# A state-space layer's inner loop on one Trainium2 core: the sums over states one scan later, softplus from one product, the skip term on VectorE, the gate multiplied by GpSimd

## The chip, the cores and the metric

One Trainium2 chip, one of its cores. The metric is the device time of the whole program in microseconds (us); here it is the median of three runs. A profile is one further execution taken by the hardware profiler. The engines are PE (TensorE, matmul), DVE (VectorE), ACT (ScalarE), POOL (GpSimd) and SP (SyncE, which here only issues DMAs). Each engine works through its own queue of instructions in order: an instruction that waits holds up all that stand behind it on that engine.

## What is computed

The program runs two transformer-like layers over 8 sequences of 1024 positions with 256 features, all in 32-bit floats. The first layer (mixture of experts, causal attention, mixture of experts) is not touched. The second is a channel mix, a selective state-space block and a second channel mix. The change is in the state-space block, cut here to what matters:

```
xz = in_proj_w @ h                       # h: normalised x; 2 x 512 channels
u, z = split(xz)
uc = silu(conv1d(u) + conv_b)            # causal, 4 taps, per channel
dt, Bm, Cm = split(x_proj_w @ uc)        # 64 + 16 + 16 rows
delta = softplus(dt_proj_w @ dt + dt_proj_b)
state[t] = exp(delta[t] * A) * state[t-1] + delta[t] * Bm[t] * uc[t]   # 512 channels x 16 states
y[t] = sum over the 16 states of state[t] * Cm[t]
y = (y + uc * D) * silu(z)
out = out_proj_w @ y + x
```

## The kernel before, in words

The second layer is `Layer1`. Its loop in `run` walks over `order`: 8 sequences b, of each 4 chunks c of 128 channels, of each chunk 16 steps k. One step holds 16 channels x 8 states on the 128 partitions and all 1024 positions along the free axis; two successive steps hold the two halves of the 16 states of the same channels. 8 x 4 x 16 makes 512 steps. Per step:

- SP fetches delta and delta*uc of 16 channels from DRAM, each row spread over 8 partitions (`fetch`, L1618; one fetch for two steps, four steps ahead; three buffers each).
- POOL multiplies by B (`feed`, L1641, two steps ahead).
- ACT computes exp(delta*A) into PSUM (`decay`, L1650, one step ahead; two buffers, so that a decay has to wait until the step two before it has been multiplied by C).
- DVE scans over the positions (L1744) and multiplies by C into `hc` (L1749; six buffers).
- Every fourth step PE adds the last four `hc` over their states into `py` (`add_up`, L1672), one PSUM tile `y` for the chunk. Before the first of these sums of a chunk a product with a diagonal matrix, `through` = D on the diagonal, made by ACT at L1757, puts uc*D into `py` (L1663).
- At step k = 1 of the next chunk, `close` multiplies `py` by silu(z), tile `zs`, into `uc` (L1683, DVE).

All other work of the layer is woven into this loop as side work. It consists of generators that yield before each small step with a rough cost (`need`): `steps_before` (mix, normalisation, projection and convolution of the next sequence), `steps_low` (B, C and the first delta of the next sequence), `steps_gate` (delta of the next chunk, then silu(z) of this one), and `steps_behind` (output projection and second mix of the sequence before). `Steps.turn` is called twice in each step of the loop and takes what is due by rates that are fixed when a list is added; `gap` is a least number of turns between two steps of a list. `drain` empties a list at once; the delta lists are drained at k = 12, where the fetches for the next chunk begin. PE products of side work use two PSUM banks (`bank`), which ACT or DVE empties one product later (`Pipe`).

Softplus is in `steps_delta`. It is computed as max(p, 0) + ln(1 + e) with e = exp(-|p|), and the rounding error of 1 + e is put back: with s = 1 + e rounded, ln s - ((s - 1) - e). The product p is made twice: first for Abs (L1466, ACT), and again at the end for the maximum (L1457 PE, L1480 DVE). In between, for each half of the 1024 positions, ACT makes s, ln s and s - 1 (L1473 to L1475) and POOL subtracts twice (L1477, L1478). One buffer of `sp1` holds s of a half. At last POOL makes du = delta*uc (L1486), and delta and du are sent to DRAM (`sent`, L1494).

The order in which add_up and the two turns stand in a step is this, before the change:

```python
            side.turn(0.5)
            if i % self.Q == 0 and i:
                add_up()
            nc.vector.tensor_tensor_scan(
                decays[i], decays[i], inputs.pop(i), 0.0, ALU.mult, ALU.add
            )
            side.turn(0.5)
            hc = pools["hc"].tile([P, T], F32, name="hc")
```

Of the kernel before, what the change touches and what calls it, by code (L numbers as in the profile page):

```python
# [8 lines left out]
F32 = mybir.dt.float32  # L9
BF16 = mybir.dt.bfloat16  # L10
I32 = mybir.dt.int32
AF = mybir.ActivationFunctionType
ALU = mybir.AluOpType
# [4 lines left out]
P = 128  # L18
# [27 lines left out]
class Net:  # L46


    def __init__(self, ctx, tc, B, T):
        self.tc, self.nc = tc, tc.nc  # L50
        self.B, self.T = B, T
        self.N = B * T
        self.NT = T // P
        self.C = self.N // P
        self.K = self.N // E
        self.KT = self.K // P
        nc = self.nc
        cp = ctx.enter_context(tc.tile_pool(name="consts", bufs=1))
        self.cp = cp
        self.ident = cp.tile([P, P], F32, name="ident")  # L60
        make_identity(nc, self.ident)
        self.ones = cp.tile([P, P], F32, name="ones")
        nc.gpsimd.memset(self.ones, 1.0)
        self.eps5 = cp.tile([P, 1], F32, name="eps5")
        nc.gpsimd.memset(self.eps5, 1e-5)
        self.eps6 = cp.tile([P, 1], F32, name="eps6")
        nc.gpsimd.memset(self.eps6, 1e-6)
# [439 lines left out]
class Attention:  # L507
# [5 lines left out]
    W = 512  # L513
# [418 lines left out]
    class Lists:  # L932
# [18 lines left out]
        def take(self, *kinds):  # L951

            for entry in self.lists:
                if entry[0] in kinds:
                    return self.step(entry)
# [106 lines left out]
class Layer1:  # L1062
# [9 lines left out]
    W = 512  # L1072
# [375 lines left out]
    def steps_delta(self, q, c, pools, pipe):  # L1448


        net, nc = self.net, self.net.nc
        T, W = net.T, self.W

        def offered(take):
            for t0 in range(0, T, W):
                pd = self.bank(pools, [P, W], "pd")
                nc.tensor.matmul(  # L1457
                    pd, self.w_dt[:, c * P : (c + 1) * P], q.xd[:, t0 : t0 + W],
                    start=True, stop=True,
                )  # L1460
                pipe.filled(lambda t0=t0, pd=pd: take(slice(t0, t0 + W), pd))

        yield need(pe=1.7, act=1.2)
        dl = pools["delta"].tile([P, T], F32, name="delta")
        e = du = pools["du"].tile([P, T], F32, name="du")
        offered(lambda t, pd: nc.scalar.activation(e[:, t], pd, AF.Abs))  # L1466
        yield need(act=1.1, banks=True)
        pipe.flush()
        nc.scalar.activation(e, e, AF.Exp, scale=-1.0)
        for t in (slice(0, W), slice(W, T)):  # L1470
            yield need(act=2.3, gap=2 if t.start else 0)
            e1 = pools["sp1"].tile([P, W], F32, name="sp_e1")
            nc.scalar.activation(e1, e[:, t], AF.Identity, bias=net.ones[:, 0:1])  # L1473
            nc.scalar.activation(dl[:, t], e1, AF.Ln)
            nc.scalar.activation(e1, e1, AF.Identity, bias=self.minus)  # L1475
            yield need(pool=2.5, gap=2)
            nc.gpsimd.tensor_tensor(e1, e1, e[:, t], ALU.subtract)  # L1477
            nc.gpsimd.tensor_tensor(dl[:, t], dl[:, t], e1, ALU.subtract)  # L1478
        yield need(pe=1.7, dve=1.4, gap=2)
        offered(lambda t, pd: nc.vector.scalar_tensor_tensor(  # L1480
            dl[:, t], pd, 0.0, dl[:, t], ALU.max, ALU.add
        ))
        yield need(banks=True, gap=1)
        pipe.flush()
        yield need(pool=2.3, gap=1)
        nc.gpsimd.tensor_tensor(du, dl, q.uc[c], ALU.mult)  # L1486
        q.steps[c] = self.sent(pools, "dl", c, dl)
        yield need(gap=1)
        q.du[c] = self.sent(pools, "du", c, du)
# [109 lines left out]
    def run(self, pools, load, load_x, keep_x, store):  # L1599
        net, nc = self.net, self.net.nc  # L1600
        T, W, B = net.T, self.W, net.B
        seqs = [self.Sequence(b) for b in range(B)]
# [51 lines left out]
        def add_up():  # L1654

            i0 = summed[0][0]
            b, c, _, _ = order[i0]
            first = i0 % NS == 0
            if first:
                self.py = pools["y"].tile([P, T], F32, name="y")  # L1660
            for t0 in range(0, T, W):
                if first:
                    nc.tensor.matmul(  # L1663
                        self.py[:, t0 : t0 + W], self.through,
                        seqs[b].uc[c][:, t0 : t0 + W], start=True, stop=False,
                    )
                for p in range(self.PARTS):
                    for i, hc in summed:
                        l, n = order[i][2:]
                        if n == p:  # L1670
                            g, j = divmod(l, self.RG // self.G)
                            nc.tensor.matmul(  # L1672
                                self.py[g * self.RG : (g + 1) * self.RG, t0 : t0 + W],
                                self.pick[:, j, :], hc[:, t0 : t0 + W], start=False,
                                stop=(j == self.RG // self.G - 1 and p == self.PARTS - 1),
                            )
            summed.clear()

        def close(i):

            b, c = order[i][:2]
            q = seqs[b]
            nc.vector.tensor_tensor(q.uc[c], self.py, q.zs, ALU.mult)  # L1683

        def before(b):

# [13 lines left out]
        side, pipe = self.Steps(), self.Pipe()  # L1700
# [12 lines left out]
        for i, (b, c, l, p) in enumerate(order):  # L1713
            k = i % NS
            if k == 2:
                if c == 0:
                    if b > 0:
                        side.drain("3behind")
                        side.add("3behind", behind(b - 1), 85, 56)
                    if b + 1 < B:  # L1720
                        side.add("2before", before(b + 1), 175, 48)
            if k == (0 if 0 < c < NDC - 1 else 2):
                side.add(
                    "1gate", self.steps_gate(seqs[b], c, pools, pipe),
                    *((30, 8) if c + 1 < NDC else (8, 2)),
                )
            if c == NDC - 1 and b + 1 < B and not seqs[b + 1].low:
                if k == 5:
                    side.drain("2before")
                if "2before" not in side.lists:  # L1730
                    seqs[b + 1].low = True
                    side.add("2low", self.steps_low(seqs[b + 1], pools, pipe), 33, 6)
            if k == NS - self.AHEAD:
                side.drain("1gate")
                if c == NDC - 1:
                    side.drain("2low")
            if p == 0:
                fetch(i + self.AHEAD)
            decay(i + 1)
            feed(i + 2)  # L1740
            side.turn(0.5)
            if i % self.Q == 0 and i:
                add_up()
            nc.vector.tensor_tensor_scan(  # L1744
                decays[i], decays[i], inputs.pop(i), 0.0, ALU.mult, ALU.add
            )
            side.turn(0.5)
            hc = pools["hc"].tile([P, T], F32, name="hc")
            nc.vector.tensor_tensor(hc, decays.pop(i), seqs[b].rep["c", p], ALU.mult)  # L1749
            summed.append((i, hc))  # L1750
            if (c, l) == (NDC - 1, lines[-1]) and b + 1 < B:
                rep(b + 1, "c", p)
            if k == 1:
                if i > 1:
                    close(i - 2)
                self.through = pools["through"].tile([P, P], F32, name="through")
                nc.scalar.mul(self.through, net.ident, self.skip[:, c : c + 1])  # L1757
        side.drain("3behind")
        add_up()
        close(len(order) - 1)  # L1760
# [5 lines left out]
def kernel(  # L1766
# [30 lines left out]
    nc = tc.nc  # L1797
    B, T, _ = x.shape
    net = Net(ctx, tc, B, T)
# [20 lines left out]
    with ExitStack() as st:  # L1820
        at = Attention(net, pool_in(st, "at_w", 1), w_qkv, w_out, b_out)
        with ExitStack() as ro:
            room = moe.room(ro)
            with ExitStack() as ph, tc.manual_schedule():
                pool, px = pool_in(ph, "f", 2), pool_in(ph, "f_x", B)
# [8 lines left out]
                while todo or works:  # L1834
                    if todo and len(works) < 2 and turn % 4 == 0:
                        b = todo.pop(0)
# [10 lines left out]
        with ExitStack() as ph:  # L1847
            at.places(pool_in(ph, "at_qk", 1), dram1)
            pools = {
                name: pool_in(ph, f"at_{name}", bufs) for name, bufs in (  # L1850
                    ("x", 3), ("xn", 2), ("xT", 1), ("side", 1), ("pT", 4), ("so", 2), ("oT", 2),
                    ("over", 2), ("sm", 2), ("junk", 1), ("r", 1), ("rT", 1),
                )
            }
# [14 lines left out]
    with ExitStack() as st:  # L1869
        w = pool_in(st, "l1_w", 1)  # L1870
# [4 lines left out]
        with tc.manual_schedule():  # L1875
            with ExitStack() as ro:
# [4 lines left out]
            name: pool_in(st, f"l1_{name}", bufs) for name, bufs in (  # L1881
                ("x", 2), ("mixT", 1), ("ka", 2), ("r", 2), ("hT", 2), ("u", 1), ("uc", 2 * NDC),
                ("xd", 1), ("delta", 1), ("du", 1), ("sp1", 1), ("zs", 1),
                ("rep", 1), ("sdl", 3), ("sdu", 3), ("dbu", 2), ("hc", 6), ("tap", 1), ("through", 1), ("xn", 2), ("small", 2),
            )
        }
        pools["dram"] = dram2
# [57 lines left out]
```

## Time and profile before

| what | value |
|---|---|
| median of 3 runs | 5593.31 us (5590.47 to 5599.83) |
| the profiled execution, its own time | 5598.68 us |
| its span in the profile | 5597.0 us |
| granted TensorE clock, mean over the span | 0.894 |
| first step's data of the second layer's loop | at about 2904 us |
| last chunk's gate | at 5524.84 us |
| one sequence of the loop, from 4237.28 to 4578.65 us | 341.37 us |

The span begins with the first instruction and ends with the last; 1.7 us of the execution's time lie outside it. A group in the profile is told by line, engine and operation, then output <- inputs by the program's names. Matmul records count more than the source: a product of 512 columns in 32-bit floats shows as two. The text speaks of steps as "c1 k4"; in the sequence of the table c0 k2 begins at 4237.28, c1 k0 at 4322.34, c2 k0 at 4405.17, c3 k0 at 4494.29, and c0 k2 of the next sequence at 4578.65 us.

### The profile page before, as it was taken

The page shows a single profiled execution, that of the slowest core. Times are in us where ns is not written, and L with a number is a line of the kernel's source. Part 1 is how long each engine was busy: PE and PEld are TensorE (multiplying, and loading weights), DVE is VectorE, ACT ScalarE, POOL GpSimd, SP SyncE. Part 2 cuts the span into 40 slices and gives each one's busy share as a digit, 9 for nine tenths or more (in the row PEclk, how much of TensorE's full clock was granted, in tenths as well). Part 3 has the DMA queues.
Part 4 walks back from the last instruction along what each step waited for, and adds up shares of the span by engine and source line. Part 5 has one row for each costly group of instructions (what it writes and reads, how often), then busy time and mean ns, then how long its engine had stood idle before and what let it go on. Part 6 is the DMA issues. An engine that isn't in the chain of part 4 may idle for free.

```text
span 5597.0 us, 60307 instructions
## 1 busy us (share of the span) xinstructions
PE 4612.8 (82%) x21302; PEld 2200.7 (39%) x21302; DVE 3432.3 (61%) x5654; ACT 2502.0 (45%) x4150; POOL 2202.1 (39%) x1801
## 2 busy tenths in 40 slices
PE   5699699999999997599767778787887878878767
PEld 5365434444444443356423233332433323333324
DVE  5532166666666773632117876777767677677884
ACT  2111145665566553011145556464564645545443
POOL 1244211111111111243226655666656555556662
PEclk7799889999999998699878889888898989989888
DMA  6123212212221222133134544536336364454642
GB/s 211 28 58 64 75 41 79 67 61 71 86 67 60 76 71 67 33 64 58 31 80 125 155 126 110 157 109 164 109 107 159 109 155 117 118 141 121 166 135 64
DMA packets 253568, 545.28 MB, mean 97 GB/s; under 512 B 30257, under 2 KB 144001, under 8 KB 253266
## 3 DMA queue, kind: packets, MB, share of 16 engines
q1 hardware_dynamic: 228690, 507.34, 32.2%
q0 software_dynamic: 24576, 34.10, 3.7%
q8 instruction: 168, 2.75, 0.2%
q14 instruction: 134, 1.10, 0.1%
HBM read 400.31 MB, written 141.03 MB: 97 GB/s over the span
## 4 chain that ended last, share of the span: by engine, by line
PE 26%; DVE 13%; ACT 6%; issue 5%; DMA 2%; POOL 1%; SPq 0%; DVEq 0%; POOLq 0%; ACTq 0%
DVE h L1744 8%; PE y L1672 5%; PE pc L1391 4%; PE pr L1286 4%; PE pk L1264 4%; PE pu L1442 2%; DVE hc L1749 2%; PE pp L1526 2%; ACT h L1650 2%; PE pd L1457 1%; ACT xn L1220 1%; PE pm L472 1%; PE px L1421 1%; DMA sdu<-du 1%; PE po L489 1%
## 5 line engine op out<-in xcount | busy, mean ns | idle before, releaser
L777 ACT ACTIVATE pT<-s 128x512 f32<-128x512 f32 (+3 forms) x1536 | 669.5, 489 | 520.2 <-PE s L734 510.8
L1650 ACT ACTIVATE h<-sdl,A 128x1024 f32<-128x1024 f32 x512 | 567.0, 1112 | 644.9 <-DVE hc L1749 623.2
L1672 PE MATMUL y<-hc,pick 128*32 128x512 f32 x2048 | 655.7, 723 | 226.9 <-DVE hc L1749 226.9
L734 PE MATMUL s<-kT,qT 32*128 32x512 f32 (+3 forms) x3072 | 828.6, 538 | 14.2 <-DVE mx L750 11.6
L1641 POOL TENSOR_TENSOR dbu<-sdu,b 128x1024 f32<-128x1024 f32 x256 | 602.0, 2352 | 409.2 <-DMA sdu<-du 215.1
L734 PE MATMUL s<-qT,kT 32*128 32x512 f32 (+3 forms) x3072 | 742.2, 538 | 7.7 <-ACT pT L777 7.7
L1744 DVE TENSOR_TENSOR_SCAN h<-h,dbu 128x1024 f32<-128x1024 f32 x256 | 586.0, 2289 | 184.7 <-ACT h L1650 158.8
L1744 DVE TENSOR_TENSOR_SCAN h<-h,sdu 128x1024 f32<-128x1024 f32 x256 | 586.1, 2289 | 159.6 <-ACT h L1650 146.4
L1749 DVE TENSOR_TENSOR hc<-h,c 128x1024 f32<-128x1024 f32 x512 | 625.5, 1222 | 31.5 <-PE y L1672 3.8
L783 POOL TENSOR_SCALAR_AFFINE_SELECT pT<-pT 128x512 f32<-128x512 f32 x256 | 162.4, 635 | 1137.0 <-ACT pT L777 1053.4
L1641 POOL TENSOR_TENSOR sdu<-sdu,b 128x1024 f32<-128x1024 f32 x256 | 602.4, 2353 | 15.8 <-DMA b<-bc 5.0
L734 PEld LDWEIGHTS s<-kT,qT 32*128 32x128 f32 x3072 | 318.9, 186 | 435.4 <-DVE mx L750 189.7
L476 ACT ACTIVATE mid<-pm,bu 128x512 f32<-128x512 f32 x192 | 131.6, 686 | 724.8 <-PE pm L472 714.7
L747 DVE TENSOR_REDUCE part<-s 128x1 f32<-128x512 f32 x512 | 329.1, 685 | 179.9 <-PE s L734 179.2
L1672 PEld LDWEIGHTS y<-hc,pick 128*32 128x32 f32 x2048 | 128.1, 126 | 718.8 <-issue 398.4
L497 POOL DMA_INDIRECT acc<-o,idx x128 | 207.1, 1618 | 496.0 <-DVE o L494 229.3
L750 DVE CUSTOM_DVE_ANT_0 junk<-s,mask,part 128x256 f32<-128x256 f32 (+3 forms) x512 | 281.5, 550 | 157.5 <-PE s L734 112.6
L472 PE MATMUL pm<-tT,wu 128*128 128x512 f32 x768 | 362.5, 609 | 0.0
L489 PE MATMUL po<-wd,mid 128*128 128x256 f32 x1536 | 350.1, 391 | 0.0
L750 DVE CUSTOM_DVE_ANT_0 junk<-s,mask 128x256 f32<-128x256 f32 (+3 forms) x512 | 250.5, 489 | 139.9 <-PE s L734 87.9
L797 PE MATMUL po<-pT,at_v 128*32 128x512 f32 (+3 forms) x3072 | 329.6, 501 | 0.7 <-POOL pT L783 0.4
L489 PEld LDWEIGHTS po<-wd,mid 128*128 128x128 f32 x1536 | 302.8, 198 | 44.5 <-issue 1.0
(262 smaller groups left out, 6703.8 us busy)
## 6 DMA issues: line engine op xcount, KB each, us to landing
sdl<-dl SPq DMA_DIRECT2D x256, 512.0 KB
sdu<-du SPq DMA_DIRECT2D x256, 512.0 KB
acc<-xt SPq DMA_DIRECT2D x24, 1024.0 KB
xt<-acc SPq DMA_DIRECT2D x24, 1024.0 KB
rows<-moe_r SPq DMA_DIRECT2D x16, 1056.0 KB
qT<-padded_q SPq DMA_DIRECT2D x32, 512.0 KB
kT<-padded_k SPq DMA_DIRECT2D x32, 512.0 KB
kept<-so SPq DMA_DIRECT2D x64, 256.0 KB
```

What stands on the lines that cost most here:

```text
L472: nc.tensor.matmul(pm, wu[:, k, n * P : (n + 1) * P], tT[:, k, t0 : t0 + HALF], start=(k == 0), stop=(k == KC - 1),)
L489: nc.tensor.matmul(po, mid[:, n, j * P : (j + 1) * P], wd[:, n, :], start=(n == 0), stop=(n == NF - 1),)
L734: self.net.nc.tensor.matmul(s[:, 0 : rhs.shape[-1]], lhsT, rhs, start=True, stop=True)
L747: nc.vector.tensor_reduce(part, sh, AX.X, ALU.max)
L750: nc.vector.tensor_tensor_reduce(junk[:, 0:w], sh[:, 0:w], self.mask[:, W - w : W], 1.0, part if a else -3e38, ALU.add, ALU.max, self.mx[n ...
L777: self.net.nc.scalar.activation(pT[:, h, 0:w], sh[:, 0:w], AF.Exp, scale=1.0 / HD**0.5)
L797: nc.tensor.matmul(q.po[h * HS : (h + 1) * HS, o:W], self.va[q.b % 2][:, j, g * HG + h, :], pT[:, h, 0 : W - o], start=(j == 0), stop=(j = ...
L1641: nc.gpsimd.tensor_tensor(inputs[i], t, seqs[b].rep["b", p], ALU.mult)
L1650: nc.scalar.activation(decays[i], spread["dl", i - p], AF.Exp, scale=self.A[:, p, n : n + 1])
L1672: nc.tensor.matmul(self.py[g * self.RG : (g + 1) * self.RG, t0 : t0 + W], self.pick[:, j, :], hc[:, t0 : t0 + W], start=False, stop=(j == ...
L1744: nc.vector.tensor_tensor_scan(decays[i], decays[i], inputs.pop(i), 0.0, ALU.mult, ALU.add)
L1749: nc.vector.tensor_tensor(hc, decays.pop(i), seqs[b].rep["c", p], ALU.mult)
```

## The change

Four edits, all in `Layer1`. The sums over states (`add_up`) are issued after the scan of their step and after the second turn. Softplus uses one product: ACT reads it for Abs and for Relu (into `dl`), the second product and the DVE operation go, and ACT and POOL work in four quarters in place of two halves, where one tile of `sp1` (of the same size, one buffer) now holds ln s and s - 1 of a quarter, and POOL adds ln s to the Relu as a third operation. The skip term leaves PE: DVE computes uc*D + py at the gate, and `through` goes. The multiplication by silu(z) follows on POOL. The `gap` values and costs of the softplus steps change with it.

```diff
-        self.ones = cp.tile([P, P], F32, name="ones")
+        self.ones = cp.tile([P, 1], F32, name="ones")
...
-        yield need(pe=1.7, act=1.2)
+        yield need(pe=1.7, act=2.4)
         dl = pools["delta"].tile([P, T], F32, name="delta")
         e = du = pools["du"].tile([P, T], F32, name="du")
-        offered(lambda t, pd: nc.scalar.activation(e[:, t], pd, AF.Abs))
-        yield need(act=1.1, banks=True)
+        for t0 in range(0, T, W):
+            pd = self.bank(pools, [P, W], "pd")
+            nc.tensor.matmul(
+                pd, self.w_dt[:, c * P : (c + 1) * P], q.xd[:, t0 : t0 + W], start=True, stop=True
+            )
+
+            def take(t=slice(t0, t0 + W), pd=pd):
+                nc.scalar.activation(e[:, t], pd, AF.Abs)
+                nc.scalar.activation(dl[:, t], pd, AF.Relu)
+
+            pipe.filled(take)
+        yield need(act=1.7, banks=True)
         pipe.flush()
         nc.scalar.activation(e, e, AF.Exp, scale=-1.0)
-        for t in (slice(0, W), slice(W, T)):
-            yield need(act=2.3, gap=2 if t.start else 0)
-            e1 = pools["sp1"].tile([P, W], F32, name="sp_e1")
-            nc.scalar.activation(e1, e[:, t], AF.Identity, bias=net.ones[:, 0:1])
-            nc.scalar.activation(dl[:, t], e1, AF.Ln)
-            nc.scalar.activation(e1, e1, AF.Identity, bias=self.minus)
-            yield need(pool=2.5, gap=2)
-            nc.gpsimd.tensor_tensor(e1, e1, e[:, t], ALU.subtract)
-            nc.gpsimd.tensor_tensor(dl[:, t], dl[:, t], e1, ALU.subtract)
-        yield need(pe=1.7, dve=1.4, gap=2)
-        offered(lambda t, pd: nc.vector.scalar_tensor_tensor(
-            dl[:, t], pd, 0.0, dl[:, t], ALU.max, ALU.add
-        ))
-        yield need(banks=True, gap=1)
-        pipe.flush()
+        w = W // 2
+        for t0 in range(0, T, w):
+            t = slice(t0, t0 + w)
+            yield need(act=1.2, gap=1 if t0 else 0)
+            e1 = pools["sp1"].tile([P, 2, w], F32, name="sp_e1")
+            nc.scalar.activation(e1[:, 0, :], e[:, t], AF.Identity, bias=net.ones[:, 0:1])
+            nc.scalar.activation(e1[:, 1, :], e1[:, 0, :], AF.Identity, bias=self.minus)
+            nc.scalar.activation(e1[:, 0, :], e1[:, 0, :], AF.Ln)
+            yield need(pool=2.2, gap=1)
+            nc.gpsimd.tensor_tensor(e1[:, 1, :], e1[:, 1, :], e[:, t], ALU.subtract)
+            nc.gpsimd.tensor_tensor(dl[:, t], dl[:, t], e1[:, 0, :], ALU.add)
+            nc.gpsimd.tensor_tensor(dl[:, t], dl[:, t], e1[:, 1, :], ALU.subtract)
         yield need(pool=2.3, gap=1)
         nc.gpsimd.tensor_tensor(du, dl, q.uc[c], ALU.mult)
...
             for t0 in range(0, T, W):
-                if first:
-                    nc.tensor.matmul(
-                        self.py[:, t0 : t0 + W], self.through,
-                        seqs[b].uc[c][:, t0 : t0 + W], start=True, stop=False,
-                    )
...
-                                self.pick[:, j, :], hc[:, t0 : t0 + W], start=False,
+                                self.pick[:, j, :], hc[:, t0 : t0 + W], start=(j == 0 and p == 0),
...
-            nc.vector.tensor_tensor(q.uc[c], self.py, q.zs, ALU.mult)
+            nc.vector.scalar_tensor_tensor(
+                q.uc[c], q.uc[c], self.skip[:, c : c + 1], self.py, ALU.mult, ALU.add
+            )
+            nc.gpsimd.tensor_tensor(q.uc[c], q.uc[c], q.zs, ALU.mult)
...
             side.turn(0.5)
-            if i % self.Q == 0 and i:
-                add_up()
             nc.vector.tensor_tensor_scan(
                 decays[i], decays[i], inputs.pop(i), 0.0, ALU.mult, ALU.add
             )
             side.turn(0.5)
+            if i % self.Q == 0 and i:
+                add_up()
...
-                self.through = pools["through"].tile([P, P], F32, name="through")
-                nc.scalar.mul(self.through, net.ident, self.skip[:, c : c + 1])
```

## The prediction

> **What bounds the kernel now.** I read the page first, then the waits and groups of one sequence in the middle of the second layer (4237.28 to 4578.65 us), then the chain of waits and the timelines inside it. The page's busy shares and the same shares for that sequence:
>
> ```profile
> PE 4612.8 (82%) x21302; PEld 2200.7 (39%) x21302; DVE 3432.3 (61%) x5654; ACT 2502.0 (45%) x4150; POOL 2202.1 (39%) x1801
> ```
> ```profile
> 4237.28:4578.65 341.37, 271.65 (x816) 118.38 (x816) 247.60 (x202) 182.17 (x243) 200.93 (x139) 0.89 0.49 130
> ```
>
> Of 341.4 us PE is busy 271.7, DVE 247.6, POOL 200.9, ACT 182.2 (then granted clock, DMA share, GB/s). Nobody is full: the loop is bound by engines that wait for each other in order. Scan and hc alone need 64 x (2.29 + 1.22) = 224.6 us of DVE, so a sequence cannot come much under 250. Who waits for whom (total us, times, longest):
>
> ```profile
> ACT h L1650 <- DVE hc L1749: 75.1, 30, 7.3
> DVE h L1744 <- ACT h L1650: 46.1, 14, 5.9
> POOL sp_e L1477 <- ACT sp_e L1475: 40.6, 6, 13.2
> PE y L1672 <- DVE hc L1749: 26.5, 9, 5.8
> ...
> POOL du L1486 <- DVE delta L1480: 17.1, 2, 9.4
> ...
> DVE uc L1683 <- PE y L1672: 11.6, 3, 7.2
> ...
> DVE delta L1480 <- PE pd L1457: 7.8, 3, 6.3
> ```
>
> DVE's dearest wait is for the next decay on ACT: 46.1 us. The first line is only a decay's two PSUM buffers, and costs nothing by itself. A decay is late when ACT stands before it with something else in hand: evicting a PE product, or softplus. So what counts is where the change puts work in ACT's queue, and when PE hands ACT its products.
>
> **What goes.** The groups of the sequence (count | busy us, mean ns of one):
>
> ```profile
> L1457 PE MATMUL pd<-xd,w_dt 97*128 97x512 f32 x32 | 17.4, 652 | 6.1 <-ACT ka L1272 4.6 <-DVE cm_r L1310 1.1 <-DVE xt L1530 0.3
> ...
> L1477 POOL TENSOR_TENSOR sp_e<-sp_e,du 128x512 f32<-128x512 f32 x8 | 10.2, 1270 | 40.6 <-ACT sp_e L1475 40.6
> ...
> L1663 PE MATMUL y<-uc,through 128*128 128x512 f32 x16 | 9.6, 685 | 1.2 <-ACT h L1650 1.2
> ...
> L1480 DVE SCALAR_TENSOR_TENSOR delta<-pd,delta 128x512 f32<-128x512 f32 x8 | 5.5, 686 | 8.3 <-PE pd L1457 7.8 <-POOL delta L1478 0.5
> ```
>
> PE loses half of pd (8.7 us) and all of through (9.6): 18.3 of 271.7. DVE loses 8 x 0.686 = 5.5. ACT loses four through of 0.393 (1.6) and the halves, 8 x (0.712 + 0.630 + 0.722) = 16.5. POOL loses 16 x 1.27 = 20.3. Most of PE's 18.3 lies beside other work; the chain of waits has these pieces of what goes: pd 1.98 and 0.88, through 1.05, 0.86 and 1.05, delta with its issue gaps 3.33, ACT's through 0.40. That is 9.55 us a sequence. One such place, c2 k4 to k6 (start, us, what):
>
> ```profile
> 4435.34 1.05 PE y L1672 x2
> 4436.38 1.05 PE y L1663 x2
> 4437.44 1.84 PE y L1672 x8
> 4439.28 7.07 PE pc L1391 x16
> 4446.35 0.88 PE pd L1457 x2
> 4447.25 0.69 DVE delta L1480
> ```
>
> **What comes.** ACT: 8 Relu from PSUM at 0.59 like Abs (4.7), and 16 quarters of Identity, Identity, Ln on 256 columns. No row has that size. Below, half of the 512 column times (1.03 a quarter); above, xn 128x256 at 0.594 each (1.78). From 512 to 1024 columns one ACT operation grows by about 0.43, so 256 is about 0.21 less than 512: 0.50 + 0.50 + 0.42 = 1.42. Sum 22.7; ACT nets +9.3 (bounds +3 to +15). POOL: 48 operations on 256 columns. Below, 0.55, which the one-input xt<-xt,n_up,n_off on 256 columns takes; above, 0.73 by the growth from 1.27 at 512 to 2.35 at 1024 columns; I take 0.73, as these have two inputs: 35.0. The gate multiply is as du, 1024 columns, 2.35: 9.4. POOL nets +24.1 (+16 below), to 225 of 341. DVE's gate changes from a two-input to a scalar-and-two-input operation: on 512 columns xt<-xt,pp takes 0.685 and cm_r<-pv,cm_r 0.678, so nothing, within 0.1. The DMAs stay: delta and du go out about as early in POOL's queue (du one feed earlier in c0 and c1), and SP's list is as long.
>
> **What is moved and who waits.** The orders in which the built programs hold their instructions give the rest; I laid the durations along them by hand.
>
> c1 (k0 to k8), a loss. In POOL's queue the gate multiply now stands ahead of the feed of k4, and the first quarter of softplus behind that feed. The multiply waits for DVE's close, and this for the sums; these now stand behind one more mix product (pk, 3.65 us) and end at about 4335.5 where they ended at 4332.0. So: close 4336.7, multiply 4339.0, feed 4341.3, first quarter 4343.4. ACT's second quarter needs the one `sp1` buffer, so it waits until then and ends at 4345. Behind it on ACT stand both sigmoid evictions, which PE has ready before that, and the decay of k4:
>
> ```profile
> 4342.62 0.60 ACT L1296 ACTIVATE cm_r<-pr 128x512 f32<-128x512 f32 x1 [1.58 <-PE pr L1286]
> 4343.24 1.28 ACT L1156 ACT_TABLE_LOAD   x1
> 4344.53 1.12 ACT L1650 ACTIVATE h<-sdl,A 128x1024 f32<-128x1024 f32 x1
> ```
>
> That decay ends at about 4350.0 in place of 4345.65: +4.4. Less the deltas and their wait there (1.8): **+2.6**. What was hidden here, POOL's 9.5 us of idle before its second half, is the cover that now decides.
>
> c2, about even. The gate multiply pushes POOL by 2.35, hidden behind ACT's table load and sigmoids (ACT wants the second quarter at 4431.3, POOL frees the buffer at 4429.2). But ACT's third quarter waits for POOL's second to about 4435, and tap, behind it, is ready at 4440 in place of 4438. PE has nothing then for 8.6 us, and the sums, issued later, cut into pc. The decay of k7 ends at about 4454 with a fast PE, against 4450.2 before; the delta waits gone (6.3 + 0.7) and PE's 3 us less pay most back by k9: -1.7. Here a rule speaks against the change. A pause of PE shows in the granted clock (third number from the end) of these windows:
>
> ```profile
> 4319.50:4324.10 4.60, 0.01 (x1) 0.00 (x0) 4.57 (x3) 2.24 (x3) 4.52 (x3) 0.97 0.33 91
> 4324.10:4326.20 2.10, 2.06 (x4) 0.56 (x6) 2.06 (x3) 1.11 (x2) 0.74 (x2) 0.50 0.85 207
> 4326.20:4332.00 5.80, 5.80 (x18) 1.25 (x17) 3.11 (x2) 5.66 (x8) 3.00 (x2) 0.62 0.49 127
> ```
>
> After 4.6 us without work PE ran at half speed for 2.1 + 0.76 x 5.8 = 6.5 us, which cost about 3.2. The Trainium skill (TensorE: Matmul & The Clock Gate, part 1, the HAM clock gate) says that PE drops to half rate after an idle window of about 3.4 us and needs about 3.4 us of work to come back: a cost of about 1.7. By the rule c2 gives -1.7 + 1.7 = 0, by the row +1.5; the row is this kernel's, I take **+1.2** as part hides. So less work on PE is partly paid in clock.
>
> c3, the gain. Before the sigmoids PE does pd 1.80, through 1.91 and the sums 3.7, then pr. Now through is gone and three quarters of pr stand ahead of the sums: pr ends 2.0 earlier, and ACT has its second softplus step (2.06) behind it in no case. The decay of k7 comes 4.1 earlier, deltas save 1.3, and POOL, with 4.4 us a step against DVE's 3.5, gives back 0.8: **-4.6**.
>
> c0, even. The quarters stand between the four xn of the mix: pp starts at about 4267.7, not 4264.15. The second pd (1.98) and the deltas after it (2.9) go, and the sums leave the front of pr; pr starts at 4296.9 against 4296.27: **+0.5**. The multiply hides under the 11 us in which POOL waits for a DMA.
>
> Sum: 2.6 + 1.2 - 4.6 + 0.5 = -0.3 a sequence, times 7: -2. The last sequence loses delta waits of 7.9 and 1.7 us and gains POOL locks of about 4 us in two chunks: about 0. At the very end the multiply stands alone before the output projection: +2.4. PE idles 18 us more a sequence; one further cold start, half of it on the path, is 1.6 x 8 = +13. Together +14: 5598.7 + 14 = 5612.7 against the profiled execution. The median of the runs is 5.4 below that execution, so 5593.3 + 14 = **5607**. About 0.2% (11 us) is what a measurement of this kernel can tell from no change.
>
> **The rivals.** *PE's relief decides.* All 9.55 us leave the chain and neither POOL nor the clock takes anything back, for which speaks that PE holds most of the chain: 8 x 9.55 = 76, 5517 (5500 to 5575). Against it: ACT's wait in c1 must not happen. *The one buffer decides, slower.* ACT's quarters wait for POOL, which waits for the gate. It decides where POOL ends its first quarter in c1 after the last sigmoid eviction could be done, 4343.2; from there each us of POOL is a us of the loop. With c1 +4.4, c2 +4.6, c0 +3.5 and less than half of c3's gain, +10 a sequence: 5673. *The later sums do nothing.* In c2 (pc, pd, sums, pr) they keep their neighbours, so the 7.2 us in which DVE waits for them at the gate stay. This is contained in the first sum, and moves it by no more than 2 us a sequence (16).
>
> **How the numbers follow.** The balance has 0.45 (own range 5580 to 5635), PE's relief 0.30, the buffer 0.25. In the balance's range about a third lies within 0.2%, a tenth below. Faster 0.34, same 0.16, slower 0.50. The range 5510 to 5680 leaves out some 0.1 on each side.
>
> **What would show it.** Right: a wait of ACT sp_e for POOL in every sequence (8.4 us in all of 3750 to 5500 before), longest in c1; POOL du no longer waiting for DVE; PE less busy by about 18 us a sequence at a lower mean clock; c3 shorter and c1 longer. Wrong: c1 not longer, or DVE's 46 us for decays fallen by a third; or PE's clock unchanged.

## The result, and the profile after

The kernel after takes 5615.59 us (median of 11 runs, 5602.99 to 5622.30) beside 5594.11 us before (11 runs, 5586.20 to 5605.51): a ratio of 1.0033, 95% interval 1.0023 to 1.0042. The medians lie 21.5 us apart; the ratio, taken over all runs, stands for about 18 us. The profiled execution after has a span of 5613.9 us, 16.9 more than the one before.

First the page's busy shares of the kernel after (us, share of the span, instructions), to be held against the first lines shown of before.

```profile
PE 4486.9 (80%) x21046; PEld 2169.7 (39%) x21046; DVE 3399.0 (61%) x5590; ACT 2562.8 (46%) x4374; POOL 2390.5 (43%) x2089
```

PE does 126 us less, DVE 33 less; ACT does 61 more and POOL 188 more. By busy shares the bound engine was relieved, and the time grew. The same sequence of the second layer, from k2 of its c0 to k2 of the next, in the row by windows with PE, PEld, DVE, ACT and POOL, then granted clock, DMA share and GB/s:

```profile
4256.60:4600.30 343.70, 259.16 (x784) 115.72 (x784) 243.41 (x194) 189.64 (x271) 223.93 (x175) 0.85 0.49 129
```

PE fell from 271.7 to 259.2 us, at a clock of 0.85 for 0.89. POOL rose from 200.9 to 223.9, ACT from 182.2 to 189.6. The length didn't fall: 343.7 for 341.4. Its waits (total us, times, longest):

```profile
DVE h L1738 <- ACT h L1648: 47.9, 16, 6.5
...
POOL uc L1679 <- DVE uc L1676: 39.2, 4, 16.6
...
ACT sp_e L1476 <- POOL delta L1482: 20.2, 6, 9.0
...
DVE uc L1676 <- PE y L1665: 15.0, 3, 7.2
```

DVE's waits for pd and POOL's for delta are gone, as the edit of softplus implies. DVE's wait for decays stayed (46.1, now 47.9, and the longest grew from 5.9 to 6.5). Two waits are new: POOL stands 39.2 us before the multiply of the gate, and ACT stands 20.2 us before a quarter of softplus until POOL gives the one buffer back. The second can hold up a decay, since decays are in ACT's queue; the first holds up what stands behind the multiply on POOL, a feed and the next quarter. The groups give the new operations' prices (count | busy us, mean ns of one | idle before them):

```profile
L1480 POOL TENSOR_TENSOR sp_e<-sp_e,du 128x256 f32<-128x256 f32 x16 | 11.6, 728 | 10.6 <-ACT sp_e L1477 10.6
...
L1476 ACT ACTIVATE sp_e<-du,ones 128x256 f32<-128x256 f32 x16 | 8.1, 504 | 20.3 <-POOL delta L1482 20.2
...
L1676 DVE SCALAR_TENSOR_TENSOR uc<-uc,skip,y 128x1024 f32<-128x1024 f32 x5 | 6.4, 1277 | 15.0 <-PE y L1665 15.0
```

The table below divides the second layer by the starts of its 512 scans. A sequence is counted from k2 of its c0 to k2 of the next c0; inside it, c0 is k2 to k15, c1 and c2 have 16 steps each, c3 has 16 and the next two. Chunk times are means of the six middle sequences.

| part, us | before | after | difference |
|---|---|---|---|
| until the first scan | 2919.0 | 2926.2 | +7.2 |
| first sequence | 290.8 | 301.9 | +11.1 |
| c0 | 85.0 | 84.1 | -0.9 |
| c1 | 82.9 | 86.9 | +4.1 |
| c2 | 89.1 | 87.7 | -1.4 |
| c3 | 84.4 | 82.7 | -1.8 |
| a middle sequence (six of them) | 341.4 | 341.5 | +0.1 |
| last sequence, k2 to its last scan | 250.9 | 247.1 | -3.8 |
| last scan to the end | 81.2 | 82.8 | +1.6 |

So six sequences break even, as a sum of a loss in c1 and gains elsewhere, and what is lost in all stands ahead of them. Of the +7.2 at the start, 3.5 is there before the first product of softplus: the first layer is the same in both programs, and in the profiles of the experiments below, which don't touch it either, the first scan came anywhere from 2914.4 to 2935.7 us. Single executions therefore can't settle the start.

### The profile page after: what moved, and what is told of

Read it like the earlier page. It is cut to its first block, busy times and chain, and to the rows that moved or that the text cites. A ratio compares the mean times of both kernels' runs of the same rounds, so it can differ in the third digit from the quotient of the medians.

```text
span 5613.9 us, 60312 instructions
## 1 busy us (share of the span) xinstructions
PE 4486.9 (80%) x21046; PEld 2169.7 (39%) x21046; DVE 3399.0 (61%) x5590; ACT 2562.8 (46%) x4374; POOL 2390.5 (43%) x2089
## 4 chain that ended last, share of the span: by engine, by line
PE 24%; DVE 9%; ACT 7%; POOL 5%; issue 5%; DMA 3%; SPq 0%; DVEq 0%; POOLq 0%; ACTq 0%
DVE h L1738 6%; PE y L1665 4%; PE pc L1391 4%; PE pk L1264 4%; PE pr L1286 3%; PE pu L1442 2%; ACT h L1648 2%; DMA sdu<-du 2%; PE pp L1524 1%; POOL dbu L1639 1%; DVE hc L1745 1%; PE pm L472 1%; PE px L1421 1%; ACT xn L1220 1%; ACT L1156 1%
## 5 line engine op out<-in xcount | busy, mean ns | idle before, releaser
L1665 PE MATMUL y<-hc,pick 128*32 128x512 f32 x2048 | 626.5, 706 | 237.8 <-DVE hc L1745 226.9
L1228 PE MATMUL tr<-ident,xn 128*128 128x128 f32 x384 | 96.9, 374 | 300.3 <-ACT xn L1220 276.1
```

The lines of the kernel that those rows point to most:

```text
L1665: nc.tensor.matmul(self.py[g * self.RG : (g + 1) * self.RG, t0 : t0 + W], self.pick[:, j, :], hc[:, t0 : t0 + W], start=(j == 0 and p == 0 ...
```

## The experiments

My theory after the result was that of the prediction: gains and a POOL lock that cancel. It had two claims that could fail: that the later sums were harmless or good, and that the lock in c1 was the multiply's. The rivals were that the later sums themselves lose, and that softplus or the gate loses by itself. So I made each of the three edits alone first. Each ran 4 to 21 times, beside before on the same chip (before's median 5600.65 for e1 to e4, and 5602.34 on another chip for e8 to e11); the profile, and so the chunk times, are of one execution each. Chunks are counted as in the table.

| kernel | median us | ratio to before (95%) | c0 | c1 | c2 | c3 | middle sequence | first sequence |
|---|---|---|---|---|---|---|---|---|
| before | 5594.11 | 1 | 85.0 | 82.9 | 89.1 | 84.4 | 341.4 | 290.8 |
| after | 5615.59 | 1.0033 (1.0023-1.0042) | 84.1 | 86.9 | 87.7 | 82.7 | 341.5 | 301.9 |
| e1 sums later, alone | 5649.45 | 1.0087 (1.0073-1.0101) | 83.7 | 84.0 | 95.8 | 84.4 | 347.8 | 295.9 |
| e2 softplus, alone | 5563.94 | 0.9933 (0.9919-0.9947) | 85.2 | 82.4 | 82.7 | 83.5 | 333.8 | 288.3 |
| e3 gate, alone | 5590.98 | 0.9981 (0.9974-0.9987) | 84.1 | 82.0 | 88.7 | 82.8 | 337.6 | 293.8 |
| e4 as e3, multiply on DVE | 5588.40 | 0.9976 (0.9967-0.9986) | 82.8 | 82.3 | 88.9 | 83.6 | 337.6 | 294.7 |
| e8 after, sums early | 5556.88 | 0.9916 (0.9902-0.9929) | 84.1 | 82.3 | 82.4 | 82.3 | 331.1 | 295.4 |
| e9 as e8, multiply on DVE | 5539.26 | 0.9887 (0.9872-0.9902) | 82.5 | 82.3 | 82.1 | 83.4 | 330.4 | 292.8 |
| e10 after, one sum early | 5581.96 | 0.9961 (0.9948-0.9975) | 83.7 | 86.8 | 81.8 | 82.5 | 334.8 | 301.1 |
| e11 after, multiply at k5 | 5591.12 | 0.9977 (0.9969-0.9986) | 84.3 | 83.3 | 87.7 | 82.6 | 338.0 | 295.3 |

**The later sums alone (e1).** Before, with one move:

```diff
-            if i % self.Q == 0 and i:
-                add_up()
             nc.vector.tensor_tensor_scan(
                 decays[i], decays[i], inputs.pop(i), 0.0, ALU.mult, ALU.add
             )
             side.turn(0.5)
+            if i % self.Q == 0 and i:
+                add_up()
```

> Before, with the sums alone issued one scan later (through and the second product stay). My theory (gains of PE in c3 are given back by waits of ACT for POOL and by what is exposed at the start): in c3 three quarters of pr now stand ahead of the sums and of through, so its evictions and the decay of k7 come about 4 us earlier in each of 7 sequences: about -25 us, 5569. Rival 'the later sums do nothing': within 8 us of 5594. Rival 'the later sums lengthen the wait at the gate': DVE uc <- PE y grows from 84 us by 3 us for most chunks and the time rises by 20 us or more.

Measured: 5649.45 us, slower by 0.87%. My expectation had the wrong sign. The rival of a longer wait at the gate had the sign, but not the place: that wait grew from 84.5 to 101.0 us in the whole program, while c2 alone grew by 6.7 us in each middle sequence; c1 grew by 1.1 and c3 not at all. PE's timeline of e1 in c2 (start, us, what, idle before):

```profile
4459.39 8.22 PE L1391 MATMUL pc<-u,tap 128*128 128x512 f32 x12 [5.68 <-ACT tap L1383]
4467.44 1.02 PE L1663 MATMUL y<-uc,through 128*128 128x512 f32 x2
...
4473.13 1.99 PE L1391 MATMUL pc<-u,tap 128*128 128x512 f32 x4
4474.95 2.06 PE L1457 MATMUL pd<-xd,w_dt 97*128 97x512 f32 x4
```

PE first waits 5.68 us for tap with nothing in its queue. Then through and the sums of k4, 5.7 us together, stand between the 12th and the 13th pass of pc, and pd behind that. DVE's timeline of e1 shows who pays:

```profile
4476.01 0.69 DVE L1480 SCALAR_TENSOR_TENSOR delta<-pd,delta 128x512 f32<-128x512 f32 x1 [13.07 <-PE pd L1457]
```

DVE stands 13.07 us for pd. Before, the sums lay ahead of pc (4437.44 and 4439.28 in the lines of the prediction), in a time in which PE had nothing else.

**Softplus from one product, alone (e2).** Before, with this part of the change (shortened here):

```diff
-            nc.gpsimd.tensor_tensor(dl[:, t], dl[:, t], e1, ALU.subtract)
-        yield need(pe=1.7, dve=1.4, gap=2)
-        offered(lambda t, pd: nc.vector.scalar_tensor_tensor(
-            dl[:, t], pd, 0.0, dl[:, t], ALU.max, ALU.add
-        ))
...
+                nc.scalar.activation(dl[:, t], pd, AF.Relu)
...
+            nc.gpsimd.tensor_tensor(dl[:, t], dl[:, t], e1[:, 0, :], ALU.add)
+            nc.gpsimd.tensor_tensor(dl[:, t], dl[:, t], e1[:, 1, :], ALU.subtract)
```

> Before, with softplus alone from one product, in quarters. My theory: PE loses 8.7 us and DVE 5.5 us a sequence, but the chain of quarters between ACT and POOL through one buffer is longer: +3.6 us at the start of the loop where nothing hides it, some +8 in sequence 0, which has little side work, and no gain in c1 or c2 of the others: together +5 to +20 us, about 5607. Rival 'PE's relief decides': -5 us a sequence, about 5555. Rival 'only the gate multiply ahead of the quarters makes them late': without it no loss, 5594 or less.

Measured: 5563.94 us, 0.67% faster. My own theory, a loss of 5 to 20 us, failed; 'PE's relief' with 5555 is near. A middle sequence gains 7.6 us, 6.4 of them in c2, where DVE no longer waits for a second pd. Of the waits of e2 in the same sequence, the one for the buffer of softplus:

```profile
ACT sp_e L1476 <- POOL delta L1482: 13.0, 6, 8.8
```

The quarters on one buffer make ACT wait 13.0 us already without any multiply on POOL, and it costs the loop nothing there: c1 is at 82.4 for 82.9.

**The gate, alone (e3, e4).** Before, with through gone, skip in DVE's operation at the gate, and the multiply on POOL in e3 (shortened):

```diff
-                if first:
-                    nc.tensor.matmul(
-                        self.py[:, t0 : t0 + W], self.through,
-                        seqs[b].uc[c][:, t0 : t0 + W], start=True, stop=False,
-                    )
...
-            nc.vector.tensor_tensor(q.uc[c], self.py, q.zs, ALU.mult)
+            nc.vector.scalar_tensor_tensor(
+                q.uc[c], q.uc[c], self.skip[:, c : c + 1], self.py, ALU.mult, ALU.add
+            )
+            nc.gpsimd.tensor_tensor(q.uc[c], q.uc[c], q.zs, ALU.mult)
```

> Before, with the skip term on DVE at the gate and the multiply by silu(z) on POOL; softplus and the place of the sums as before. My theory: through leaves PE (9.6 us a sequence, 3.4 on the chain of waits) and the multiply hides on POOL except 2.4 us at the very end, since the halves of softplus come later in POOL's queue than the quarters do: -10 to -25 us, about 5575. Rival 'the gate multiply alone makes POOL late': +10 us or more, with POOL uc waiting long for DVE uc and decays late behind softplus.

e4 has `nc.vector.tensor_tensor` in the last line.

> As the run before, but the multiply by silu(z) also on DVE, right behind the skip term. Against e3 it moves 4 x 2.35 us a sequence from POOL to 4 x 1.22 us on DVE. My theory: half of the 4.9 us of DVE is on the path, about 2.4 x 8 = +19 over e3, so about 5590 to 5595. If POOL's multiply is what costs, e4 is faster than e3 by 10 us or more. If DVE bounds most of the loop, e4 is slower than e3 by up to 39 us.

Measured: 0.9981 and 0.9976, whose intervals overlap. For e3 this is the small end of what I expected; for e4 neither my +19 us nor either rival came. Without through a middle sequence gains 3.7 us in e3 and 3.8 in e4, near the 3.36 us that through and its weights had on the chain of waits (1.05, 0.86, 1.05 and 0.40). Where the multiply stands made no difference that these runs can tell, with before's softplus.

**The change without the later sums (e8, e9).** After, with the sums back ahead of the scan; e9 also has the multiply on DVE:

```diff
-            nc.gpsimd.tensor_tensor(q.uc[c], q.uc[c], q.zs, ALU.mult)
+            nc.vector.tensor_tensor(q.uc[c], q.uc[c], q.zs, ALU.mult)
...
+            if i % self.Q == 0 and i:
+                add_up()
             nc.vector.tensor_tensor_scan(
                 decays[i], decays[i], inputs.pop(i), 0.0, ALU.mult, ALU.add
             )
             side.turn(0.5)
-            if i % self.Q == 0 and i:
-                add_up()
```

> After, with the sums back before the scan: softplus from one product and the skip and gate edits stay. Theory now: the later sums are the loss, in c2 where they cut pc in two and in c1 where they delay the gate and so POOL. Then the two other edits add up, 0.9933 x 0.9981 = 0.991 of before, about 5550; c1 near 83 us and c2 near 82.5 in a middle sequence. Rival 'the multiply on POOL and the quarters lock each other whatever the place of the sums': c1 stays at 86 to 87 us, ratio 0.995 or more. Rival 'the parts overlap': both gains are the same gain, ratio 0.993.

> As the run before, with the multiply by silu(z) on DVE behind the skip term. From e4 against e3 (no difference that can be told): the same as e8 within 0.1%, about 0.991. If POOL's multiply still holds up the quarters of softplus, it is faster than e8, by 3 us a sequence, 0.987. If DVE is the bound once PE is relieved, slower by up to 39 us.

Measured: 0.9916, as expected, and 0.9887, which is between what I expected of e9 and its first rival. Softplus and the gate add up: 0.9933 x 0.9981 = 0.9914. So the later sums carry the whole loss: on top of e8 they cost 1.0033 / 0.9916 = 1.0118, where alone they cost 1.0087. By chunks, e8 to after is 0.0, +4.6, +5.3 and +0.4 us; e1 alone was -1.3, +1.1, +6.7 and 0.0. The loss in c2 is the same one in both; that in c1 appears only with the other two edits. In the same sequence of e9, the fastest of all, DVE's wait for decays fell to 38.1 us, none over 4.2, and ACT's for the buffer to 9.5. Yet its middle sequences are only 0.7 us shorter than e8's; most of what it gains in the profile lies in the first sequence (2.6), the last (5.6) and the end (2.3), which I haven't taken apart.

**One sum early (e10).** After, where only the sum at k4 of c2 goes ahead of its scan again:

```diff
+            now = k == 4 and c == 2
+            if now:
+                add_up()
             nc.vector.tensor_tensor_scan(
                 decays[i], decays[i], inputs.pop(i), 0.0, ALU.mult, ALU.add
             )
             side.turn(0.5)
-            if i % self.Q == 0 and i:
+            if i % self.Q == 0 and i and not now:
                 add_up()
```

> After, with one of the 16 sums of a sequence back before its scan, that of c2 k4. Theory: this one sum stands in the middle of a convolution product (pc) and costs about 5 us in c2 of seven sequences: c2 from 87.7 to about 83, ratio 1.003 - 0.006 = 0.997. Rival 'all the later sums cost a little': one sixteenth of the loss comes back, ratio 1.002, c2 within 1 us of 87.7.

Measured: 0.9961, c2 at 81.8, all other parts within 0.8 us of after's but the start. One of 16 sums in a sequence was worth 5.9 us of it. PE's timeline in c2, first of after, then of e10:

```profile
4454.74 1.88 PE L1442 MATMUL pu<-hT,w_in 128*128 128x512 f32 x4
4463.92 6.89 PE L1391 MATMUL pc<-u,tap 128*128 128x512 f32 x12 [7.30 <-ACT tap L1383]
4470.74 3.63 PE L1665 MATMUL y<-hc,pick 128*32 128x512 f32 x16
4474.30 1.99 PE L1391 MATMUL pc<-u,tap 128*128 128x512 f32 x4
```

```profile
4441.60 1.88 PE L1442 MATMUL pu<-hT,w_in 128*128 128x512 f32 x4
4443.41 1.91 PE L1665 MATMUL y<-hc,pick 128*32 128x512 f32 x6
4446.82 2.76 PE L1665 MATMUL y<-hc,pick 128*32 128x512 f32 x10 [1.51 <-DVE hc L1748]
4450.78 7.11 PE L1391 MATMUL pc<-u,tap 128*128 128x512 f32 x16 [1.20 <-ACT tap L1383]
```

Tap comes at the same point in both: 4463.92 - 4454.74 = 9.18 us after the start of pu in after, 4450.78 - 4441.60 = 9.18 in e10. In e10 the sums fill that wait; in after PE idles through it and does the sums when pc is wanted. pc's last pass ends 21.5 us after pu's start (4476.29) for 16.3 (4457.89). Of these 5.3 us about 3.6 are the sums in the middle, and up to 1.8 are pc itself, which took 6.89 + 1.99 for 7.11. The windows of after say why pc took longer:

```profile
4456.60:4463.90 7.30, 0.02 (x1) 0.01 (x1) 7.23 (x5) 5.87 (x12) 7.14 (x8) 0.74 0.56 147
4463.90:4467.30 3.40, 3.38 (x5) 1.59 (x6) 3.06 (x3) 3.32 (x8) 3.40 (x3) 0.55 0.02 5
```

After 7.3 us without work PE was granted 0.55 for 3.4 us (and 1.00 in the 3.4 us that follow): 3.4 x 0.45 = 1.5 us lost. In e10 the clock is 1.00 all through pc. ACT and DVE of after show who feels it:

```profile
4476.32 0.69 ACT L1400 ACTIVATE uc<-pc,conv_b 128x512 f32<-128x512 f32 x1 [6.50 <-PE pc L1391]
...
4478.32 1.12 ACT L1648 ACTIVATE h<-sdl,A 128x1024 f32<-128x1024 f32 x1
```

```profile
4473.54 1.23 DVE L1745 TENSOR_TENSOR hc<-h,c 128x1024 f32<-128x1024 f32 x1 [4.10 <-PE y L1665]
4479.54 2.30 DVE L1738 TENSOR_TENSOR_SCAN h<-h,sdu 128x1024 f32<-128x1024 f32 x1 [4.77 <-ACT h L1648]
```

ACT waits 6.50 us for pc before it evicts it, the decay follows at 4478.32, and the scan at 4479.54 has waited 4.77 us for that. The late sums reach DVE by a second path too: they had not yet read the old `hc`, so the product by C stood 4.10 us for them (a free one of the six buffers). That wait is covered by the other, as the next scan needs the decay that follows pc. At this place of e10 DVE waits 3.51 us once, for the decay, in place of 4.10 + 4.77: the difference is 5.4.

**The multiply out of the way (e11).** After, where POOL's multiply is queued at k5 in place of k1 in c1 and c2, the same work at a later place (shortened):

```diff
-            nc.gpsimd.tensor_tensor(q.uc[c], q.uc[c], q.zs, ALU.mult)
+            gated.append((q.uc[c], q.zs))
+
+        def gate():
+
+            uc, zs = gated.pop()
+            nc.gpsimd.tensor_tensor(uc, uc, zs, ALU.mult)
...
+            if gated and k == (5 if c in (1, 2) else 1):
+                gate()
```

> After, with POOL's multiply at the gate issued at k5 in place of k1 in chunks 1 and 2 (the skip term on DVE stays at k1), behind the quarters of softplus. Theory: in c1 the first quarter on POOL ends 2.35 us earlier and ACT with it, so c1 falls from 86.8 to about 84.5 us and the ratio from 1.003 to about 1.000. Rival 'the late close alone holds c1 back' or 'the quarters lock by themselves': c1 stays within 0.7 us, ratio 1.003.

Measured: 0.9977, c1 at 83.3. That was more than I expected: 3.6 us a sequence in c1, and the first sequence at 295.3 for 301.9. The lock, in c1 of after, as POOL, ACT and DVE show it in turn:

```profile
4357.20 2.35 POOL L1679 TENSOR_TENSOR uc<-uc,zs 128x1024 f32<-128x1024 f32 x1 [12.43 <-DVE uc L1676]
...
4363.31 0.73 POOL L1482 TENSOR_TENSOR delta<-delta,sp_e 128x256 f32<-128x256 f32 x1
```

```profile
4364.07 0.51 ACT L1476 ACTIVATE sp_e<-du,ones 128x256 f32<-128x256 f32 x1 [7.12 <-POOL delta L1482]
...
4366.88 1.08 ACT L1296 ACTIVATE cm_r<-pr 128x512 f32<-128x512 f32 x2
...
4369.28 1.12 ACT L1648 ACTIVATE h<-sdl,A 128x1024 f32<-128x1024 f32 x1
```

```profile
4355.78 1.28 DVE L1676 SCALAR_TENSOR_TENSOR uc<-uc,skip,y 128x1024 f32<-128x1024 f32 x1 [6.16 <-PE y L1665]
...
4370.50 2.30 DVE L1738 TENSOR_TENSOR_SCAN h<-h,dbu 128x1024 f32<-128x1024 f32 x1 [6.51 <-ACT h L1648]
```

DVE waits 6.16 us for y; POOL therefore waits 12.43 before the multiply, and the feed (from 4359.51, 2.35 us) and the three operations of the first quarter (from 4361.83) are behind it; ACT waits 7.12 for the quarter's buffer, and both sigmoids and the decay are behind that; DVE waits 6.51 for the decay. ACT in the same place in e11:

```profile
4336.91 0.51 ACT L1476 ACTIVATE sp_e<-du,ones 128x256 f32<-128x256 f32 x1 [0.88 <-POOL delta L1482]
...
4341.95 0.60 ACT L1296 ACTIVATE cm_r<-pr 128x512 f32<-128x512 f32 x1 [1.64 <-PE pr L1286]
...
4343.86 1.12 ACT L1649 ACTIVATE h<-sdl,A 128x1024 f32<-128x1024 f32 x1
```

The wait is 0.88 us, and the sigmoids wait for PE again, as before. The close still comes late there (DVE stood 5.44 us for y), so the late close alone isn't what holds c1 back. With e10 this accounts for the middle sequences, if the two gains add, which was not run: 341.5 - 6.7 (e10) - 3.5 (e11) = 331.3, and e8, which has all the sums early, measures 331.1.

## Why the prediction was right, point by point

Sign and size held: +14 predicted, +18 measured. The lock in c1 was foreseen link by link. The total is luck. Its terms are -2 + 2.4 + 13 (13.4, put down as 14), and the 13 are for cold starts that the runs don't show as a cost. The 16.9 us between the two profiles come chiefly from places that I had counted at about nothing: 7.2 before the first scan and 11.1 in the first sequence.

- **Prices.** Right. Quarters of 0.504, 0.508 and 0.416 us on ACT for 0.50, 0.50 and 0.42; 0.73 us on POOL for 0.73; the multiply 2.35. The gate's operation on DVE took 1.277 us where it took 1.222 before, inside the 0.1 allowed.
- **c1, the lock.** Right in mechanism, too small: +4.1 for +2.6. Late sums, close, multiply, feed, quarter, ACT, sigmoids, decay: each link is in the lines above, and e11 and e8 each take it away. It needs its parts together: the three edits alone change c1 by +1.1, -0.5 and -0.9.
- **c2, about even.** The number is near (-1.4 for +1.2) and two larger terms were missed. Softplus alone gains 6.4 there; the late sum takes 5.9 of it back. I had seen that PE would have nothing to do and that the sums would cut into pc; I did not count that the sums had been filling that very gap.
- **c3.** -4.6 predicted, -1.8 measured, and the reason was wrong: the sums behind pr give nothing (84.4 to 84.4 in e1). The gain is softplus' and the gate's (-0.9 and -1.6 alone).
- **c0.** +0.5 predicted, -0.9 measured. ACT's longest wait for POOL, 9.03 us, lies here and not in c1 as I had said; c1's is 7.12. c0 is shorter all the same.
- **Sum of a sequence.** -0.3 predicted, +0.1 measured, by luck: the four chunks were off by +1.5 (c1), -2.6 (c2), +2.8 (c3) and -1.4 (c0).
- **The first sequence.** I counted it like the others; it lost 11.1 us. e11 takes 6.6 of that back and e8 takes 6.5. The rest, some 4.5, I haven't divided further; e8 has it too, and the gate alone (e3) lengthens this sequence by 3.0.
- **The start.** Counted at nothing. From the first pd to the start of du it took 17.9 us for 14.3: the quarters there run in single file, ACT waiting 1.94 us for POOL in each turn. The +3.6 lies within the spread of first scans, so its share in the medians is open.
- **The last sequence and the end.** 0 and +2.4 predicted, -3.8 and +1.6 measured.
- **Cold starts, +13.** The further cold start failed as a cost. The mean clock fell as said (0.894 to 0.878). By the clock records of the traces, PE worked at half clock long enough to lose about 28.4 us a middle sequence for 27.0 before; but e8 loses 28.8 and still gains 10.3 us a sequence, where the pieces on the chain promised 9.55. The cold start in c2, which I had counted apart, did come. There the loss was 1.5 us, near the 1.7 that I estimated by the Trainium skill (TensorE: Matmul & The Clock Gate, part 1), and not the 3.2 of the row that I preferred; the last section shows why the two differ.
- **The signs.** ACT's wait for POOL came (103.1 us from 3750 to 5500 us, where 8.4 stood before), POOL's for DVE before du went, c1 grew and c3 shrank, DVE's 46 us for decays stayed. PE's load fell by 12.5 us in the sequence shown, for 18.

Of the rivals, *PE's relief* describes two of the three edits: its 9.55 us a sequence are 10.3 in e8. I gave the whole 0.30 and never asked which edit would keep it from happening. *The later sums do nothing* is false: they are what loses. What I should have done is to price each edit alone along the queues before laying them together. The range held the time.

Not tried: a second buffer for the quarters, or halves from one product. What the single buffer costs, apart from the order in the queues, is therefore not shown.

## What to carry to other kernels

Where an in-order engine has a gap while it waits for another, look at what fills it before moving that work later: here one group of sums, moved from a 7.3 us gap into the middle of the product awaited next, cost 5.9 us of a sequence while PE's load fell. When a change has several edits, lay the queues out for each alone: two gained 0.67% and 0.19%, the third lost 0.87% alone and 1.2% with them, as its delay met a multiply and a single buffer in another queue. Where an operation stands in the way of what is awaited, a place a few steps later in the queue may be enough: e11 took about 0.6% off with the same operations.

## What was not expected of the hardware

The cost of a pause differed within one kernel, and the shorter pause cost more: about 3.2 us after 4.6 us of idle in before's c1, 1.5 after 7.3 us in after's c2. Finer windows show why. First before, then after (span, busy PE, PEld, DVE, ACT, POOL, then the granted clock):

```profile
4319.50:4323.80 4.30, 0.01 (x1) 0.00 (x0) 4.26 (x3) 1.96 (x3) 4.22 (x3) 1.00 0.28 79
4323.85:4330.65 6.80, 6.51 (x14) 1.61 (x16) 5.42 (x4) 5.66 (x9) 3.07 (x2) 0.50 0.61 157
```

```profile
4456.60:4460.10 3.50, 0.02 (x1) 0.00 (x0) 3.47 (x3) 2.14 (x5) 3.42 (x5) 1.00 0.64 163
4460.15:4463.90 3.75, 0.00 (x0) 0.01 (x1) 3.71 (x3) 3.69 (x8) 3.67 (x4) 0.50 0.49 132
4463.90:4466.95 3.05, 3.03 (x4) 1.50 (x5) 2.90 (x2) 2.99 (x7) 3.05 (x3) 0.50 0.02 5
```

In both the clock was halved for the same 6.8 us, from 4323.83 to 4330.65 and from 4460.12 to 4466.95. In before PE's work began 0.3 us into that stretch, so 6.5 us of it were worked at half speed. In after PE stayed idle for its first 3.8 us, and 3.0 us of work were left to pay. What these pauses cost is half of the part of the stretch that falls on work. In the clock records of all ten traces the share is 1.0 or 0.5 and nothing else, and it changes only after whole multiples of 3.41 us, the first and the last stretch apart.

And the mean granted clock said little about time: 0.894 before, 0.884 in the fastest kernel, e9, whose PE is busy 4513.4 us for 4612.8.
